# Moving four projections of a two-layer attention kernel from the score loop to the value stage, with narrower bias products and tokens that carry their own ones

## The chip, the cores and the metric

The kernel runs on one core of a Trainium2 chip. The metric is device time in microseconds (us) of one execution, the median of several. The core has a matrix engine (TensorE, "PE" in the profile, with its weight loads listed apart as "PEld"), VectorE ("DVE"), ScalarE ("ACT"), GpSimd ("POOL") and a queue engine that issues transfers ("SP"). TensorE writes its results to PSUM, which is divided into banks of 512 fp32 columns; VectorE and ScalarE read them from there. All data are fp32. A matmul of fp32 shows in the trace as two passes, each with its own weight load.

## The reference, cut to what matters

Sixteen images of 64 x 64 positions and 256 channels go through two layers, each with a residual:

```python
# layer 0: linear attention on the group-normalised input
q, k, v = split(gn(x) @ w_qkv)            # 8 heads of 32
q = softmax(q, over the 32 of a head) * 32**-0.5
k = softmax(k, over all 4096 positions)
context = einsum('bhdn,bhen->bhde', k, v)
x = x + einsum('bhde,bhdn->bhen', context, q) @ w_out

# layer 1: attention in a 7 x 7 window on the group-normalised result
q, k, v = gn(x) @ Wq + bq, gn(x) @ Wk + bk, gn(x) @ Wv + bv
scores = sum over d of q[d] * (unfolded k[d] + emb[d])     # 49 neighbours
x = x + sum over neighbours of softmax(scores) * unfolded v
```

`gn` is a group norm with 32 groups, without scale or shift. `emb` is a position embedding: one half depends on the row offset of the neighbour, the other on its column offset.

## The kernel before, in words

The work of one image comes in three stages. The order of instructions on TensorE, ScalarE, VectorE and SP is the order in which the program writes them (`manual_schedule`, L1170); the instructions of GpSimd are not in that list. A tile framework adds the waits between engines.

**Layer 0** (`layer0`, L576). Sixteen pieces of 256 positions are projected (L592), exponentiated by ScalarE (L596) and summed into a 256 x 257 context per half of the heads (L610). The right side of that product are the *tokens*: the unnormalised input, position by position, with a 257th column of ones, so that the last column of the context is the sum of the keys' exponentials. `load_tokens` (L519) writes the ones with GpSimd (L522) and loads the rest from the array `xt` in HBM (L523); the tokens of an image are loaded in pieces, beside the last attention steps of the image before and during layer 0. Context, value weights and output weights are then multiplied together to one weight per head (L660 to L683); VectorE and ScalarE copy the result from PSUM to `w4` (L707, L708), and the products L733 with these weights give layer 0's output, four heads at a time on four row tiles.

**Values** (L1212 to L1260). The group norm is not applied to the image: its scale is multiplied into the weights (`scale`, L761), and its mean is taken off through the bias. `fold_bias` (L765) computes for each of the five bias columns the product of the scaled weights with the mean (L772) and subtracts it (L774): columns 0 and 1 are the keys', 2 and 3 the queries', 4 belongs to the position products. The position products (L790) are placed by ScalarE, stored to HBM and read back as rings. Then the eight strips of 512 positions get their value products (L854), in the order `KEYED`; VectorE adds the bias (L863), and the result goes to HBM. The loop index over `KEYED` is i = 0 to 7; the bias products of keys and queries stand in i = 2.

The keys and queries of the window attention are made in *jobs*. A key job `("k", hg, s)` makes keys for half `hg` of the heads and strip `s`: 2 matmuls of 512 columns, 4 passes. A query job `("q", hg, t, half)` makes a quarter `t` of the columns, one half of the rows: 6 matmuls of 96 to 256 columns, 12 passes. Both are at L902 (`job_products`, L877). `place_job` (L910) moves a job's bank from PSUM to SBUF with its bias, in one instruction per head (two for strip 0, whose positions lie in two pieces); `evacuate` (L776) does it on ScalarE (L779) or on VectorE (L781). `AHEAD` (L47) names the jobs made among the values, placed by ScalarE; `JOBS` (L48) those made among the attention steps, and `placements` (L82) says, by the remainder of the step number by five, in which step each engine places which heads, ahead of that step's scores (`FIRST`) or behind them (`LAST`).

**Window attention** (`local_attention`, L947). A round k of eight makes one quarter of one half of the heads (`SEQUENCE`); a round has nine chunks in five groups, so 40 steps, with two chunks a step and one in each fifth. Three things run at once, one step apart. In step n, group n gets its scores (L990), and ScalarE exponentiates them (L999 or L1002); the scores of all chunks alternate between two double banks, so a chunk's scores wait for the exponential of the chunk before last. Group n - 1 is multiplied with the values (L1034) into two output banks, `single[0]` and `single[1]`, which are cleared at the start of a round (L1045) and copied by ScalarE at its end (L1133); VectorE then adds the overlap of neighbouring chunks (L1019). Group n - 2 is summed (L1073) into `single[2]`, which VectorE transposes out of the bank (L1079) and inverts (L1081). Jobs use `single[2]` or `single[3]`: a job of step n with n % 5 = 3 stands ahead of the value products and uses `single[3]`; one in `single[2]` stands behind them, and where n % 5 = 0 and there is a job of step n + 1, that one follows it at once in `single[3]`.

So four lists set the order around the change: TensorE's, ScalarE's, VectorE's and SP's. `load_window` (L935) brings the values of a round to SBUF through SP; `load_rings` (L830) the position rings.

Of the kernel before, what the change touches and what calls it, by code (L numbers as in the profile page):

```python
# [19 lines left out]
P = 128  # L20
W = 64
C = 256
HEADS, HD = 8, 32
NS = 8
# [21 lines left out]
SUMS = ((0, 18), (18, 42), (42, 64))  # L46
AHEAD = {3: (("k", 0, 2), ("k", 0, 3)), 4: (("k", 0, 4),), 5: (("q", 0, 1, 0),), 6: (("q", 0, 1, 1),), 7: (("k", 0, 5),)}  # L47
JOBS = {  # L48
    0: ("k", 0, 6),
    1: ("q", 0, 2, 0),  # L50
    2: ("q", 0, 2, 1),
    3: ("k", 0, 7),
    5: ("q", 0, 3, 0),
    6: ("k", 0, 0),
    7: ("q", 0, 3, 1),
    8: ("k", 0, 1),
# [22 lines left out]
FIRST, LAST = 0, 1  # L79


def placements():  # L82

    plan = {}
    for n, job in JOBS.items():
        if job[0] == "k" and job[2] == 0:
            parts = ((0, LAST, 1, (2, 3)), (1, FIRST, 0, (0, 1)))
        elif n == max(JOBS):
            parts = ((0, LAST, 1, (0, 1)), (1, LAST, 1, (2, 3)))
        elif n % 5 == 1:  # L90
            parts = ((0, LAST, 1, (0, 1)), (1, FIRST, 0, (2, 3)))
        elif n % 5 == 3:
            parts = ((1, FIRST, 1, (0, 1)), (2, FIRST, 0, (2, 3)))
        elif n % 5 == 0:
            parts = ((1, FIRST, 1, (0, 1)), (1, FIRST, 0, (2, 3)))
        else:
            parts = ((1, FIRST, 1, (0, 1, 2, 3)),)
        for later, when, engine, heads in parts:
            plan.setdefault((n + later, when), []).append((n, engine, heads))
    return plan  # L100
# [335 lines left out]
def attention_fast(tc, io, ok):  # L436


    nc = tc.nc
    with ExitStack() as ctx:  # L440
# [15 lines left out]
        B = xc.shape[0]  # L456
# [7 lines left out]
        n = Net(tc, cp, io)  # L464
# [54 lines left out]
        def load_tokens(b, q, t0=0, t1=8):  # L519

            t = tokens_of(q)
            nc.gpsimd.memset(t[:, t0:t1, C : C + 1], 1.0)  # L522
            nc.sync.dma_start(t[:, t0:t1, :C], xt[b, q, :, t0:t1])  # L523

# [51 lines left out]
        def layer0(b, x, xn, mean, rstd, ready, midway=None):  # L576
# [128 lines left out]
            w4 = vbuf[0][:, : 8 * C].rearrange("p (h g c) -> p h g c", h=4, g=2)  # L705
            for h in range(2):
                nc.vector.tensor_copy(w4[:, h].rearrange("p g c -> p (g c)"), double[0][:, h])  # L707
            nc.scalar.copy(w4[:, 2:4].rearrange("p h g c -> p h (g c)"), double[1])  # L708
# [56 lines left out]
        def fold_bias(mean, folded, psum):  # L765

            for i, weights in folded:
                for a in range(2 if i == 4 else 1):
                    rows = slice(64 * a, 64 * a + 64) if i == 4 else slice(0, P)
                    for k in range(2):  # L770
                        w = weights[:, k] if i == 4 else weights[:, k, P * (i % 2) : P * (i % 2) + P]
                        nc.tensor.matmul(psum[rows, i : i + 1], w, mean[:, k : k + 1], start=(k == 0), stop=(k == 1))  # L772
            span = slice(folded[0][0], folded[-1][0] + 1)
# [396 lines left out]
        with tc.manual_schedule(engines=ORDERED):  # L1170
# [40 lines left out]
            for b in range(B):  # L1211
# [25 lines left out]
                for i in range(4):  # L1237
                    positional(i, pairs[i])
                spares = iter(single + single[:2])
                for i, s in enumerate(KEYED):  # L1240
# [12 lines left out]
                    if i in (3, 4):  # L1253
                        load_rings(32 * (i - 3), 32 * (i - 2))
                    for job in AHEAD.get(i, ()):
                        bank_of = next(spares)
                        job_products(job, x, bank_of)
                        place_job(job, bank_of, 1)
                    if i == 5:
# [84 lines left out]
def attention_general(tc, io):  # L1344

    nc = tc.nc
    with ExitStack() as ctx:
# [80 lines left out]
        def image(src, tokens, dst):  # L1428
# [35 lines left out]
            for s in range(NS):  # L1464
                xtok = tok.tile([P, 4, C], F32, tag="xtok", name=f"gxtok{s}")
                i = ORDER.index(s)
                nc.sync.dma_start(xtok, tokens[i // 2, :, 4 * (i % 2) : 4 * (i % 2) + 4])
                for hg in range(2):
# [249 lines left out]
```

## Time and profile before

| | us |
|---|---|
| median of 3 runs | 5167.11 (5166.51 to 5168.44) |
| profiled execution | 5175.71 |
| its span, first to last instruction | 5173.9 |

| engine | busy us | share of the span |
|---|---|---|
| PE | 5061.7 | 98% |
| PEld | 3751.8 | 73% |
| DVE | 3013.1 | 58% |
| ACT | 2571.2 | 50% |
| POOL | 1447.9 | 28% |

The granted clock of TensorE was 0.997 over the span. One image takes about 320 us. In one of them the stage from the bias of the position products to the end of the values runs from 1131.3 to 1170.4 us, and the window attention begins at 1170.4. In a timeline a row gives the start, the length of the merged run, engine, line, operation, output and inputs, shape and count; in brackets stands the idle time of that engine before the row and what ended it. Runs of TensorE are pipelined, so a run's length reaches into the next one; its cost is the difference between starts. In a list of waits the numbers are total us, times, and the longest.

### The profile page before, as it was taken

What the parts mean: (1) busy time and instruction counts of PE and PEld (TensorE: products, weight loads), DVE (VectorE), ACT (ScalarE), POOL (GpSimd) and SP (SyncE); (2) the same over time, 40 slices, a digit from 0 to 9 for tenths busy, and PEclk for the clock granted to TensorE, in tenths of its full rate; (3) what the DMA queues carried; (4) which work ended last, traced back from release to release, by engine and by line L of the source; (5) the groups of instructions that cost most, each with busy time, mean ns of one, the idle gap of its engine ahead of it and who ended that gap; (6) DMA issues with size and microseconds to landing.
All of it is one profiled execution on the core that took longest, in us unless ns stands there. A gap on an engine that the chain in (4) does not pass through costs nothing.

```text
span 5173.9 us, 175006 instructions
## 1 busy us (share of the span) xinstructions
PE 5061.7 (98%) x76273; PEld 3751.8 (73%) x76273; DVE 3013.1 (58%) x5754; ACT 2571.2 (50%) x3473; POOL 1447.9 (28%) x2630
## 2 busy tenths in 40 slices
PE   7999999999999999999999999999999999999998
PEld 4776867777677776777767677676776767767676
DVE  5474655646556465564755647556475564755546
ACT  1562735527265372653726537174471744717446
POOL 3041241412414123140331403314042140422404
PEclk9999999999999999999999999999999999999999
DMA  4542525425154351543415434153441534416343
GB/s 132 128 122 52 151 66 123 121 56 150 60 132 117 68 144 50 134 117 76 134 50 137 118 82 133 46 139 111 93 125 44 151 98 103 128 39 150 91 93 90
DMA packets 637705, 537.33 MB, mean 104 GB/s; under 512 B 129585, under 2 KB 570545, under 8 KB 632177
## 3 DMA queue, kind: packets, MB, share of 16 engines
q1 hardware_dynamic: 595712, 515.94, 37.5%
q10 hardware_dynamic: 41216, 10.10, 1.2%
q8 instruction: 602, 9.86, 0.8%
q14 instruction: 175, 1.43, 0.1%
HBM read 367.11 MB, written 158.73 MB: 102 GB/s over the span
## 4 chain that ended last, share of the span: by engine, by line
PE 96%; DVE 2%; issue 1%; POOL 0%; ACT 0%; DMA 0%; SPq 0%; POOLq 0%; ACTq 0%; DVEq 0%
PE ps L902 18%; PE pd L592 17%; PE pd L990 16%; PE ps L1034 9%; PE pd L854 9%; PE ps L610 8%; PE ps L1073 4%; PE ps L733 4%; PE pd L733 4%; PE ps L790 2%; PE ps L1045 1%; PE ps L772 1%; DVE qq L781 0%; PE pd L683 0%; PE pd L1235 0%
## 5 line engine op out<-in xcount | busy, mean ns | idle before, releaser
L779 ACT ACTIVATE qq<-ps,bias 32x512 f32<-32x512 f32 (+2 forms) x928 | 678.8, 737 | 836.9 <-DVE bias L774 649.6
L1019 DVE TENSOR_TENSOR e<-e,e 128x384 f32<-128x384 f32 x1024 | 697.9, 711 | 416.5 <-PE ps L1034 337.3
L592 PE MATMUL pd<-wqkv,img 128*128 128x512 f32 x2048 | 926.9, 595 | 8.3 <-DVE img L363 8.3
L596 ACT ACTIVATE eq<-pd 128x1024 f32<-128x1024 f32 x256 | 262.2, 1024 | 1063.9 <-PE pd L592 1063.9
L990 PE MATMUL pd<-qq,kaug 64*64 64x84 f32 (+5 forms) x24192 | 764.1, 267 | 10.8 <-issue 9.8
L990 PEld LDWEIGHTS pd<-qq,kaug 64*64 64x64 f32 x24192 | 671.4, 133 | 126.6 <-issue 72.4
L505 POOL TENSOR_TENSOR others<-others,turn 128x9 f32<-128x9 f32 (+2 forms) x384 | 86.9, 226 | 2118.6 <-DVE turn L1079 2117.8
L592 PEld LDWEIGHTS pd<-wqkv,img 128*128 128x128 f32 x2048 | 387.4, 190 | 394.2 <-issue 350.1
L599 DVE TENSOR_REDUCE qz<-eq 128x16 f32<-128x512 f32 x256 | 175.6, 686 | 714.0 <-ACT eq L596 709.3
L1002 ACT ACTIVATE e<-pd 128x896 f32<-128x896 f32 (+2 forms) x576 | 467.4, 835 | 234.1 <-PE pd L990 153.7
L779 ACT ACTIVATE kaug<-ps,bias 32x512 f32<-32x512 f32 (+2 forms) x768 | 490.3, 648 | 143.9 <-PE ps L902 80.4
L1034 PE MATMUL ps<-e,vbuf 128*32 128x112 f32 (+1 forms) x18432 | 533.3, 252 | 10.7 <-issue 10.6
L999 ACT ACTIVATE e<-pd 128x896 f32<-128x896 f32 (+2 forms) x576 | 465.4, 834 | 149.3 <-PE pd L990 72.2
L902 PE MATMUL ps<-img,wqn 128*128 128x160 f32 (+2 forms) x3072 | 523.4, 320 | 1.0 <-issue 1.0
L902 PEld LDWEIGHTS ps<-img,wqn 128*128 128x128 f32 x3072 | 470.7, 189 | 73.4 <-issue 15.0
L610 PEld LDWEIGHTS ps<-vbuf,eq 128*128 128x128 f32 x2048 | 385.1, 190 | 155.1 <-issue 100.0
L902 PE MATMUL ps<-img,w 128*128 128x512 f32 x1024 | 496.1, 609 | 1.4
L1108 POOL TENSOR_TENSOR img<-img,r 128x320 f32<-128x320 f32 (+1 forms) x512 | 495.2, 993 | 5.0
L610 PE MATMUL ps<-vbuf,eq 128*128 128x257 f32 x2048 | 489.5, 381 | 4.7 <-ACT eq L596 4.7
L1034 PEld LDWEIGHTS ps<-e,vbuf 128*32 128x32 f32 x18432 | 389.9, 109 | 142.2 <-issue 102.0
L854 PE MATMUL pd<-wvn,img 128*128 128x256 f32 x2048 | 468.2, 382 | 4.0 <-DVE hve L358 4.0
L854 PEld LDWEIGHTS pd<-wvn,img 128*128 128x128 f32 x2048 | 382.9, 190 | 67.8 <-issue 15.3
(146 smaller groups left out, 5672.0 us busy)
## 6 DMA issues: line engine op xcount, KB each, us to landing
vbuf<-vpad SPq DMA_DIRECT2D x1152, 96.0 KB
out<-img SPq DMA_DIRECT2D x256, 256.0 KB
vpad<-v SPq DMA_DIRECT2D x112, 512.0 KB
vbuf<-in_xt SPq DMA_DIRECT2D x158, 256.0 KB
img<-in_xc SPq DMA_DIRECT2D x75, 512.0 KB
img<-in_xc SPq DMA_DIRECT2D x106, 256.0 KB
qq<-pos SPq DMA_DIRECT2D x192, 128.0 KB
vbuf<-in_xt SPq DMA_DIRECT2D x60, 384.0 KB
```

The costliest lines, as they stand in the source:

```text
L592: nc.tensor.matmul(ps[:, t], xn[k][:, n0 : n0 + P], n.wqkv_sb[:, k, : 2 * C], start=(k == 0), stop=(k == 1))
L610: nc.tensor.matmul(pc[hg][:, : C + 1], eq[p][:, t, C + hg * P : C + (hg + 1) * P], tokens_of(p // 4)[:, 2 * (p % 4) + t], start=(p == 0 an ...
L733: nc.tensor.matmul(py[a], w4[rows, h, hg, co * P : (co + 1) * P], qv[rows, 4 * hg + h, 8 * HD * i : 8 * HD * (i + 1)], start=(h == 0 and h ...
L779: nc.scalar.activation(dst, src, AF.Identity, bias=bias)
L854: nc.tensor.matmul(pi[:, t], x[k][:, n0 : n0 + P], wv[:, k], start=(k == 0 and t == 0), stop=(k == 1 and t == 1))
L902: nc.tensor.matmul(dst, (wq if what == "q" else wk)[:, k, hg * P : (hg + 1) * P], part(x[k]), start=(k == 0 and i == 0), stop=(k == 1 and ...
L990: nc.tensor.matmul(to, kaug[pl][rows, u, 8 * c : 8 * c + 8].rearrange("p r w -> p (r w)"), q, start=True, stop=True,)
L999: nc.scalar.activation(e.rearrange("p (a n) -> p a n", a=2), ps[:, :, : 2 * m], AF.Exp)
L1002: nc.scalar.activation(e.rearrange("p (x r) -> p x r", r=hi - lo), src, AF.Exp)
L1019: nc.vector.tensor_tensor(part, part, rows_of(hg, c - 1, before, r0, 8 * c), ALU.add)
L1034: nc.tensor.matmul(dst, stationary, pr, **flags)
L1108: nc.gpsimd.tensor_tensor(yv, xv, by_rows(add[:, :, a - w0 : e - w0], xv), ALU.add)
```

## The change

The tables of jobs change. Four jobs, key strips 6 and 7 and both halves of query quarter 2 of the first half of the heads, are made among the values, each right behind a job that was there already. `AHEAD` now says for each job which engine places it: the first of a step of the loop ScalarE (1), the second VectorE (0). In i = 3, where two jobs stood, the second is now placed by VectorE. The banks are taken in turn: `single` twice and its first two once more. In the attention steps the later jobs move up: query quarter 3 from steps 5 and 7 to 2 and 5, key strip 0 from step 6 to step 3. For a strip 0 in a step with n % 5 = 3 there is a placement rule of its own: VectorE places heads 0 and 1 ahead of the next step's scores, ScalarE heads 2 and 3 behind them.

`fold_bias` writes 32 output rows at a time instead of 128 (or 64 for column 4), the four groups of rows in turn. The ones come with the tokens from HBM, and the GpSimd memset goes. The first of the copies to `w4` is divided between VectorE and ScalarE.

```diff
-AHEAD = {3: (("k", 0, 2), ("k", 0, 3)), 4: (("k", 0, 4),), 5: (("q", 0, 1, 0),), 6: (("q", 0, 1, 1),), 7: (("k", 0, 5),)}
+AHEAD = {
+    3: (("k", 0, 2, 1), ("k", 0, 3, 0)),
+    4: (("k", 0, 4, 1), ("k", 0, 6, 0)),
+    5: (("q", 0, 1, 0, 1), ("q", 0, 2, 0, 0)),
+    6: (("q", 0, 1, 1, 1), ("q", 0, 2, 1, 0)),
+    7: (("k", 0, 5, 1), ("k", 0, 7, 0)),
+}
 JOBS = {
-    0: ("k", 0, 6),
-    1: ("q", 0, 2, 0),
-    2: ("q", 0, 2, 1),
-    3: ("k", 0, 7),
-    5: ("q", 0, 3, 0),
-    6: ("k", 0, 0),
-    7: ("q", 0, 3, 1),
+    2: ("q", 0, 3, 0),
+    3: ("k", 0, 0),
+    5: ("q", 0, 3, 1),
     8: ("k", 0, 1),
...
-        if job[0] == "k" and job[2] == 0:
+        if job[0] == "k" and job[2] == 0 and n % 5 == 3:
+            parts = ((1, FIRST, 0, (0, 1)), (1, LAST, 1, (2, 3)))
+        elif job[0] == "k" and job[2] == 0:
             parts = ((0, LAST, 1, (2, 3)), (1, FIRST, 0, (0, 1)))
...
             t = tokens_of(q)
-            nc.gpsimd.memset(t[:, t0:t1, C : C + 1], 1.0)
-            nc.sync.dma_start(t[:, t0:t1, :C], xt[b, q, :, t0:t1])
+            nc.sync.dma_start(t[:, t0:t1], xt[b, q, :, t0:t1])
...
-            for h in range(2):
-                nc.vector.tensor_copy(w4[:, h].rearrange("p g c -> p (g c)"), double[0][:, h])
+            nc.vector.tensor_copy(w4[:, 0, 0], double[0][:, 0, :C])
+            nc.scalar.copy(w4[:, 0, 1], double[0][:, 0, C:])
+            nc.vector.tensor_copy(w4[:, 1].rearrange("p g c -> p (g c)"), double[0][:, 1])
             nc.scalar.copy(w4[:, 2:4].rearrange("p h g c -> p h (g c)"), double[1])
...
             for i, weights in folded:
-                for a in range(2 if i == 4 else 1):
-                    rows = slice(64 * a, 64 * a + 64) if i == 4 else slice(0, P)
-                    for k in range(2):
-                        w = weights[:, k] if i == 4 else weights[:, k, P * (i % 2) : P * (i % 2) + P]
-                        nc.tensor.matmul(psum[rows, i : i + 1], w, mean[:, k : k + 1], start=(k == 0), stop=(k == 1))
+                first = P * (i % 2) if i < 4 else 0
+                for k in range(2):
+                    for q in range(4):
+                        c0 = first + HD * (q if i < 4 else q % 2)
+                        nc.tensor.matmul(
+                            psum[HD * q : HD * q + HD, i : i + 1],
+                            weights[:, k, c0 : c0 + HD],
+                            mean[:, k : k + 1],
+                            start=(k == 0),
+                            stop=(k == 1),
+                        )
...
-                spares = iter(single + single[:2])
+                spares = iter(single + single + single[:2])
...
-                    for job in AHEAD.get(i, ()):
+                    for *job, engine in AHEAD.get(i, ()):
                         bank_of = next(spares)
                         job_products(job, x, bank_of)
-                        place_job(job, bank_of, 1)
+                        place_job(job, bank_of, engine)
...
-        "xt": np.ascontiguousarray(tiles.transpose(0, 1, 3, 2, 4)),
+        "xt": np.concatenate([tiles.transpose(0, 1, 3, 2, 4), np.ones((B, NS // 2, P, 8, 1), np.float32)], axis=4),
```

More of the change, by code (lines that the diff above doesn't have):

```diff
@@ L1466, in image @@
                 i = ORDER.index(s)
-                nc.sync.dma_start(xtok, tokens[i // 2, :, 4 * (i % 2) : 4 * (i % 2) + 4])
+                nc.sync.dma_start(xtok, tokens[i // 2, :, 4 * (i % 2) : 4 * (i % 2) + 4, :C])
                 for hg in range(2):
```

## The prediction

> **What bounds the kernel now.** I read the page first (busy time, then the chain that ended last), then one image on TensorE's timeline, then the waits, then ScalarE and VectorE around the same instants.
>
> ```profile
> PE 5061.7 (98%) x76273; PEld 3751.8 (73%) x76273; DVE 3013.1 (58%) x5754; ACT 2571.2 (50%) x3473; POOL 1447.9 (28%) x2630
> PE 96%; DVE 2%; issue 1%; POOL 0%; ACT 0%; DMA 0%; SPq 0%; POOLq 0%; ACTq 0%; DVEq 0%
> ```
>
> TensorE is busy 98% and is 96% of the chain. A change can win only by making TensorE's list shorter or removing one of its few pauses, and it loses whatever new pauses it makes. So I price everything in TensorE time, from one image start to the next start (a run's own duration overlaps its successor). One image, TensorE's timeline:
>
> ```profile
> 1140.69 0.95 PE L772 MATMUL ps<-hmean,w 128*128 128x1 f32 x8
> 1141.50 1.03 PE L772 MATMUL ps<-hmean,wqn 128*128 128x1 f32 x8
> 1142.39 3.70 PE L854 MATMUL pd<-wvn,img 128*128 128x256 f32 x16
> ...
> 1152.81 1.88 PE L902 MATMUL ps<-img,w 128*128 128x512 f32 x4
> 1154.53 3.62 PE L854 MATMUL pd<-wvn,img 128*128 128x256 f32 x16
> ...
> 1171.77 1.98 PE L902 MATMUL ps<-img,w 128*128 128x512 f32 x4
> 1173.59 1.99 PE L902 MATMUL ps<-img,wqn 128*128 128x160 f32 x12
> 1175.51 1.57 PE L990 MATMUL pd<-qq,kaug 64*64 64x112 f32 x48
> ...
> 1190.79 0.38 PE L1034 MATMUL ps<-e,vbuf 128*32 128x48 f32 x16
> 1191.10 2.09 PE L902 MATMUL ps<-img,wqn 128*128 128x160 f32 x12
> 1193.02 1.91 PE L902 MATMUL ps<-img,w 128*128 128x512 f32 x4
> 1194.86 1.56 PE L990 MATMUL pd<-qq,kaug 64*64 64x112 f32 x48
> ```
>
> The first two rows are the bias products: 16 passes (each fp32 matmul shows as two) take 1.70 us, 106 ns a pass, for one column each: that is weight loading. The L902 rows are the projections ("jobs"): 1.72 us among the values (1152.81 to 1154.53), 1.82 to 2.02 among the scores, where the array changes its tile shape around them.
>
> ```profile
> DVE kaug L781 <- ACT kaug L779: 137.7, 48, 6.0
> DVE qq L781 <- ACT qq L779: 106.4, 80, 2.1
> PE ps L733 <- DVE vbuf L707: 12.5, 16, 0.8
> ```
>
> When ScalarE and VectorE share the placing of one bank, VectorE waits for ScalarE to end (first two rows): the two halves of a placement run one after the other. The third row is a pause of 0.78 us per image before the output products.
>
> **The change, part by part (per image, 16 images).**
>
> *Bias products.* For keys and queries 8 matmuls become 32, each on a 32-column tile, four tiles in turn: 64 passes for 16. The nearest row with 32-column tiles and few columns is the L1034 row at 1190.79: 16 passes in 0.31 us to the next start, the change of shape at its end included, so at most 19 ns each. Within it four neighbours run at once; 48 columns cost each tile about 42 ns, and one column should cost less. The other side: four 32-column loads take 106/4 = 27 ns if they overlap. So 64 passes are 16 rounds of 27 to 42 ns, 0.43 to 0.67 us; with about 0.2 us for two changes of shape (0.07 to enter, 0.13 to leave, as around L1034) I take 0.75, a gain of 0.95 (0.83 to 1.08). A rule speaks against it: the Trainium skill, "TensorE: Matmul & The Clock Gate", Back-to-back issue gap, gives a floor of about 25 ns to any matmul of 1 to 64 columns. By it 64 x 25 ns + 0.2 = 1.80, a loss of 0.10. The 19 ns row already lies under that floor, so I go by the row and keep the rule as the far end. The position biases (4 matmuls to 8) stay at zero: 8 passes took 0.40 us, 16 half as wide take as much, and VectorE's bias (0.25 us pause before L1235) ends the wait as before.
>
> *First copy of the output weights.* VectorE's first 512 columns (686 ns) become 256 on VectorE (about 0.42, as L1236 at 421 ns) and 256 on ScalarE. TensorE's first products need only VectorE's half: the 0.78 us pause shrinks by 0.27. ScalarE's half, behind VectorE's in the same bank, ends about 0.4 us later, when TensorE has 0.54 us of work on the first half; its next copy (1012 ns) then ends about 0.5 us before it is needed. Gain 0.27; if ScalarE's start slips, 0.
>
> *Tokens.* The ones arrive by DMA, so 14 POOL memsets of 0.1 us per image go; each stood in POOL's queue ahead of the rescaling and waited for window reads. SP issues the same number of loads, 0.4% more bytes in longer runs. TensorE waits for neither; zero. If tokens came late, the context products would wait, but the trace has no such row.
>
> *The jobs.* Before: key strips 6 and 7 and query quarter 2 (two halves) are made in steps 0 to 3; the change makes them among the values and lets the later jobs move up. Steps lose: at step 0, 1.82 + 1.92 and one change of shape (1.36 of scores to L902 at 1171.77, against 1.23 to more scores), 0.15; at step 5, where a query and a key job become one query job, 1.75; at step 7, 2.02. Sum 7.66. The values gain 2 x 1.72 + 2 x 1.83 = 7.09. Gross gain 0.57. VectorE places the four (4 x 0.76 = 3.0 us each) during the next strip's 3.45 us of value products, so values are not held up.
>
> Those jobs also covered other engines. Three waits come due:
>
> ```profile
> 1170.51 2.76 ACT L779 ACTIVATE kaug<-ps,bias 32x512 f32<-32x512 f32 x4 [2.44 <-PE ps L902]
> 1173.30 1.41 ACT L999 ACTIVATE e<-pd 128x512 f32<-128x512 f32 x2
> ```
> ```profile
> 1188.19 0.22 DVE L1081 RECIPROCAL rc<-turn 128x9 f32<-128x9 f32 x1
> 1188.66 1.03 DVE L1019 TENSOR_TENSOR e<-e,e 128x384 f32<-128x384 f32 x2 [0.26 <-PE ps L1034]
> 1189.60 0.58 DVE L1079 STREAM_TRANSPOSE turn<-ps 128x384 f32<-128x384 f32 x1
> ...
> 1194.63 1.52 DVE L781 TENSOR_SCALAR qq<-ps,bias 32x512 f32<-32x512 f32 x2 [2.06 <-ACT qq L779]
> ```
>
> (1) *Steps 0 and 1.* ScalarE places key strip 5 for 2.76 us before the first exponentials. Scores began at 1170.41; the first exponential ends at 1173.30 + 0.60. In the new order 1.72 us of key strip 7 lies in between, so that end is 1.77 us after the scores begin. Scores alone reach the third chunk, which needs that buffer, after 1.23 (0.50 and 0.73 for the two chunks before it, from their starts): wait 0.6, and 0.12 more at the fourth chunk. Queued behind: everything on TensorE. Before, 3.7 us of jobs hid it. **0.73**.
>
> (2) *Step 5.* Key strip 0 moves from step 6 to step 3, and its rule puts VectorE's half first in step 4 (four pieces, 1.71 us where it stands now), ahead of the overlap additions (1188.66) and the transpose that frees the sums bank (to 1190.18). The query job at 1191.10 writes that bank. The transpose ends at 1191.67, the job starts at 1191.73: **0.63**.
>
> (3) *Step 6.* That job's placement (ScalarE 1.37, then VectorE 1.52) must end before the last sums go into the bank. Until now 1.84 us of key job followed; without it TensorE is there 2.45 us after the job's end, and the halves need 3.03. ScalarE also comes late: its half of strip 0 follows VectorE's half (one bank), so exponentials and the two output copies end 0.5 us after the job does. **1.1**.
>
> A second rule weighs here: "PSUM — Partial Sum Buffer", PSUM bank collisions, lets two engines read one bank in different 32-partition quadrants. Under it the halves would overlap and wait 3 would be gone (jobs +0.8 instead of +1.9). The L781 waits say this kernel serialises by bank; I go by them. That ScalarE also waits for VectorE, in that order, no row shows.
>
> Jobs: 7.09 - 7.66 + 0.73 + 0.63 + 1.1 = +1.89. Instruction supply: TensorE has rare pauses marked "issue" on the scores (some 20 us in the run); denser steps and 112 more instructions, 0 to 0.3, I take 0.1.
>
> **Sum:** 1.89 - 0.95 - 0.27 + 0.10 = +0.77 us per image, x16 = +12.3. The profiled execution took 5175.7 (span 5173.9) and would take 5188; the same added to the runs' median, 5167.1, is **5179.5**.
>
> **The rivals.**
> - *The step 4 to 6 waits halve* because ScalarE need not wait for VectorE or the halves overlap: 0.5 to 1.1 less, +0.3 to -0.3; middle about 5168. For it: quadrants differ. Against: 128 waits of VectorE on ScalarE.
> - *Faster.* The sums bank is never waited for in steps 5 and 6: 1.73 less, -0.96 x 16 = -15, 5152. It decides at two points: VectorE's half of strip 0 would have to take under 1.1 us, or stand behind the transpose, and the query's halves under 2.4 us together. Against: 1.71, and 2.9.
> - *Bias products gain nothing* (the 25 ns rule, or fetching instructions for 64 short passes): +1.05 x 16 = 17 more, 5196.
> - *Nothing moves*: the jobs' gross gain is only 0.57 and TensorE's list is otherwise equal; this is the first rival's number.
>
> **How the numbers follow.** A difference under 0.2% (10 us) is what a measurement here can hardly tell from none. Main case 0.55 (5171 to 5188; above 5177.4 in three of four), halved waits 0.22 (mostly within 0.2%), faster 0.10, no bias gain 0.13. Slower 0.41 + 0.02 + 0.13 = 0.56; faster 0.09; same 0.35. The range 5158 to 5197 leaves out the faster rival and the far end of the dearest, about 0.15 to 0.2; the likeliest case's own range is 5171 to 5188.
>
> **What would show it.** In the changed profile: L772 for keys and queries as 64 passes in 0.6 to 0.9 us; TensorE's pause at L733 down from 0.78 to about 0.5; new rows of TensorE waiting for ScalarE's exponentials (L999) of about 0.7 us at step 1, for VectorE's transpose (L1079) of 0.6 at a query job in step 5, and for VectorE's placement (L781) of 1.1 at the sums (L1073) in step 6, each 16 times. The prediction is wrong if those rows are missing, if L772 stays near 1.7 us, or if the value products wait for VectorE's placements.

## The result, and the profile after

The changed kernel takes 5190.32 us (median of 4 runs, 5187.94 to 5196.36); the kernel before took 5167.77 us beside it. The ratio is 1.0040, with a 95% interval of 1.0028 to 1.0053: slower by 22.5 us (14 to 27 by the interval), where the prediction had 12.3. The profiled execution took 5196.4 us (span 5194.5), 20.7 us more than the profiled one of before; both lie above the medians of their kernels, by 6 and 8 us.

The busy times of the changed kernel:

```profile
PE 5050.5 (97%) x77169; PEld 3721.2 (72%) x77169; DVE 3181.5 (61%) x5978; ACT 2422.6 (47%) x3265; POOL 1453.5 (28%) x2410
```

TensorE works 11 us less than before (5050.5 against 5061.7) and the kernel still ends 21 us later. So the loss lies in TensorE's pauses. VectorE has 168 us more to do and ScalarE 149 us less: part of the placing went from one to the other.

The chain that ended last can't be followed in the changed kernel's profile: it breaks off at GpSimd's last instructions.

TensorE's timeline in the same image as the one shown of before (start, duration, engine, line, operation; in brackets the idle time ahead and what ended it):

```profile
1140.77 0.43 PE L776 MATMUL ps<-hmean,w 128*32 128x1 f32 x32
1141.04 0.44 PE L776 MATMUL ps<-hmean,wqn 128*32 128x1 f32 x32
1141.41 3.72 PE L864 MATMUL pd<-wvn,img 128*128 128x256 f32 x16
...
1158.74 3.84 PE L912 MATMUL ps<-img,wqn 128*128 128x160 f32 x24
1162.42 3.65 PE L864 MATMUL pd<-wvn,img 128*128 128x256 f32 x16
...
1178.41 1.86 PE L1000 MATMUL pd<-qq,kaug 64*64 64x112 f32 x48 [0.39 <-ACT e L1009]
...
1193.93 0.52 PE L1044 MATMUL ps<-e,vbuf 128*32 128x48 f32 x16
1194.94 2.09 PE L912 MATMUL ps<-img,wqn 128*128 128x160 f32 x12 [0.49 <-DVE turn L1089]
...
1198.78 0.81 PE L1044 MATMUL ps<-e,vbuf 128*32 128x64 f32 x32
1200.47 0.81 PE L1083 MATMUL ps<-e,ones 128*32 128x128 f32 x24 [0.88 <-DVE qq L791]
...
1209.01 0.97 PE L1044 MATMUL ps<-e,vbuf 128*32 128x112 f32 x32
1210.14 0.86 PE L1083 MATMUL ps<-e,ones 128*32 128x128 f32 x24 [0.16 <-DVE turn L1089]
```

The bias products now go from 1140.77 to 1141.41, 0.64 us for 64 passes where 16 took 1.70. Then come the three waits that the prediction named: at the scores of step 1, at the query job of step 5, at the sums of step 6. The last two rows are a fourth that it did not name: the sums of step 9 start 1.13 us after the products ahead of them. The kernel before needs 0.79 there:

```profile
1207.85 0.97 PE L1034 MATMUL ps<-e,vbuf 128*32 128x112 f32 x32
1208.64 0.84 PE L1073 MATMUL ps<-e,ones 128*32 128x128 f32 x24
```

TensorE's waits, summed over the run (total us, times, longest):

```profile
PE ps L1083 <- DVE qq L791: 14.2, 16, 0.9
PE ps L912 <- DVE turn L1089: 9.8, 16, 0.6
PE ps L737 <- DVE vbuf L709: 8.3, 16, 0.6
PE ps L1083 <- DVE turn L1089: 6.8, 23, 0.9
PE pd L1000 <- ACT e L1009: 6.2, 16, 0.4
```

Four of the rows come sixteen times, once per image. The fourth row mixes the wait of step 9 with others of the same kind (the kernel before has 4.9 us there, 14 times). The third row is the pause at the output weights; the kernel before had it at 12.5. In these rows a wait counts only while the array is idle, so each time lost is a little more than its row. The table below takes it from the distance between the starts of TensorE's runs instead, as a mean over 15 images. Each row is the difference of the changed kernel from the kernel before at that place, counted from the start of the image (the position biases' bias products):

```
place in an image                                   difference, us   the prediction's steps up to there
start of step 0's scores                              +6.13            +7.09 - 0.95 = +6.14
start of step 1's products (wait 1)                   +2.98            +3.0
start of step 6's products (wait 2)                   +1.89            +1.9
start of step 11's products (wait 3, then step 9)     +1.31            +0.9
start of the output products (first copy)             +0.91            +0.8
next image                                            +1.28            +0.77
```

Until step 6 the forecast holds to 0.1 us. It falls short by 0.4 us between steps 6 and 11 and by 0.3 to 0.4 us from the output products to the next image; between these two places about 0.25 us came back, which the experiment on the tokens bears on. Of the 0.37 us behind the output products' start, 0.27 is the first copy (see its experiment); the other 0.10 stands ahead of the position biases, whose products begin 0.10 us later behind the position products when they write 32 rows at a time, in the changed kernel and with the bias products alone. They end 0.06 us sooner, so this place costs 0.04 where the prediction had zero.

VectorE's and ScalarE's waits for each other at the placements:

```profile
DVE qq L791 <- ACT qq L789: 111.9, 64, 3.3
DVE kaug L791 <- ACT kaug L789: 42.7, 32, 2.7
```
```profile
ACT kaug L789 <- DVE kaug L791: 24.8, 16, 1.6
```

The last row is new: ScalarE waits 1.55 us per image for VectorE's half of key strip 0, which now stands first.

### The profile page after: what moved, and what is told of

Read it like the earlier page. It is cut to its first block, busy times and chain, and to the rows that moved or that the text cites. A ratio compares the mean times of both kernels' runs of the same rounds, so it can differ in the third digit from the quotient of the medians.

```text
span 5194.5 us, 176637 instructions
## 1 busy us (share of the span) xinstructions
PE 5050.5 (97%) x77169; PEld 3721.2 (72%) x77169; DVE 3181.5 (61%) x5978; ACT 2422.6 (47%) x3265; POOL 1453.5 (28%) x2410
## 5 line engine op out<-in xcount | busy, mean ns | idle before, releaser
L789 ACT ACTIVATE qq<-ps,bias 32x512 f32<-32x512 f32 (+1 forms) x832 | 613.7, 744 | 888.3 <-DVE bias L784 639.2
L789 ACT ACTIVATE kaug<-ps,bias 32x512 f32<-32x512 f32 (+2 forms) x640 | 403.4, 642 | 196.3 <-PE ps L912 110.9
L791 DVE TENSOR_SCALAR kaug<-ps,bias 32x512 f32<-32x512 f32 (+2 forms) x512 | 341.7, 677 | 152.6 <-PE ps L912 69.8
```

The costliest lines, as they stand in the source:

```text
L789: nc.scalar.activation(dst, src, AF.Identity, bias=bias)
L791: nc.vector.tensor_scalar(dst, src, bias, None, ALU.add)
```

## The experiments

Each kernel is timed against the kernel before on the same chip; a number of us over or under the kernel before is the difference of the two medians. Where two kernels' intervals overlap, as those of the changed kernel and of most of its variants do, the trace decides and not the time.

**One part alone.** Four kernels, each the kernel before with one part of the change.

First the bias products:

```diff
+                first = P * (i % 2) if i < 4 else 0
+                for k in range(2):
+                    for q in range(4):
+                        c0 = first + HD * (q if i < 4 else q % 2)
...
```

> The kernel before with the new bias products alone. Theory (the traces of before and after): the 64 short passes take 0.64 us where 16 took 1.70, the neighbouring runs lose 0.11, so 0.95 us per image less, and up to 0.06 at the position biases: 15 to 16 us under the kernel before. Rival (what is saved there is given back at the next wait, or the 25 ns floor of the rule holds once the cover of the jobs is gone): within 3 us of the kernel before.

Measured: 5161.52 us, 8.9 under the kernel before; ratio 0.9982 (0.9973 to 0.9990). Its TensorE timeline around the products, in the same image:

```profile
1131.52 0.43 PE L772 MATMUL ps<-hmean,w 128*32 128x1 f32 x32
1131.79 0.44 PE L772 MATMUL ps<-hmean,wqn 128*32 128x1 f32 x32
1132.16 3.72 PE L860 MATMUL pd<-wvn,img 128*128 128x256 f32 x16
```

0.64 us again. TensorE is 1.0 us ahead of the kernel before at the start of the first step, and still 0.9 to 1.1 ahead at steps 6 and 11 and at the next image; its profiled execution is 14.9 us shorter than that of before. The timed gain is smaller than 15, with an interval of 5 to 14 us. So the expected time was missed by a little, while every place in the trace has about the full microsecond. The 14.9 of the two profiled executions can't settle it, since the one of before was itself 5.3 us slower than the median it is compared with. Where the remainder goes is not shown; pauses that differ from run to run (see the tokens) may be part of it. The rival, no gain, is out.

Then the jobs, with their banks and placements:

```diff
-    0: ("k", 0, 6),
-    1: ("q", 0, 2, 0),
-    2: ("q", 0, 2, 1),
-    3: ("k", 0, 7),
-    5: ("q", 0, 3, 0),
-    6: ("k", 0, 0),
-    7: ("q", 0, 3, 1),
+    2: ("q", 0, 3, 0),
+    3: ("k", 0, 0),
+    5: ("q", 0, 3, 1),
...
```

> The kernel before with the moved projections and their placements alone. Theory: gross gain 0.57 per image, three waits of 0.70, 0.70 and 1.07, and the wait of the sums in step 9 for VectorE's transpose, 0.39, together +2.3 per image: 36 us over the kernel before (30 to 40), with all four waits at their sizes of the changed kernel. Rival A (the step 9 wait does not come from the jobs): +1.9, 30 us, and no wait at step 9. Rival B (one of the waits comes from the shorter bias products, which bring the whole stage forward): under 25 us.

Measured: 5209.18 us, 38.8 over the kernel before; ratio 1.0073 (1.0059 to 1.0086). All four waits are there. At the start of step 11's products it is 2.24 us per image behind the kernel before, times 16 is 36 us. (Its profiled execution was its fastest, 5200.0 us, and at the next image only 1.49 behind; the difference arises in the later steps.) Rival A would be 0.39 per image less, and rival B falls because the waits have the same size without the shorter bias products. The jobs cost more than the whole change does; the other parts win some of it back.

The first copy of the output weights:

```diff
-            for h in range(2):
-                nc.vector.tensor_copy(w4[:, h].rearrange("p g c -> p (g c)"), double[0][:, h])
+            nc.vector.tensor_copy(w4[:, 0, 0], double[0][:, 0, :C])
+            nc.scalar.copy(w4[:, 0, 1], double[0][:, 0, C:])
+            nc.vector.tensor_copy(w4[:, 1].rearrange("p g c -> p (g c)"), double[0][:, 1])
```

> The kernel before with the split first copy of the output weights alone. Theory: the pause ahead of the output products shrinks from 0.78 to 0.52 us, but VectorE's next copy waits for ScalarE's half and TensorE for that copy, so the stage as a whole gains nothing: within 2 us of the kernel before, with the wait of TensorE for the second copy 16 times at 0.4 us. Rival (the prediction's own step): 0.27 per image less, 4.3 us.

Measured: 5170.22 us, 0.2 under the kernel before; ratio 0.9998 (0.9990 to 1.0006). The stage begins 0.26 us earlier and is 0.27 us longer. In the kernel before VectorE makes its two copies without a wait between them:

```profile
1408.62 1.29 DVE L707 COPY vbuf<-pd 128x512 f32<-128x512 f32 x2 [0.67 <-PE pd L683]
```

The copies and the weight load behind them, in the changed kernel:

```profile
1412.03 0.43 DVE L709 COPY vbuf<-pd 128x256 f32<-128x256 f32 x1 [0.67 <-PE pd L686]
1412.49 0.37 ACT L710 COPY vbuf<-pd 128x256 f32<-128x256 f32 x1 [6.90 <-DVE vbuf L709]
...
1412.90 0.69 DVE L711 COPY vbuf<-pd 128x512 f32<-128x512 f32 x1 [0.44 <-ACT vbuf L710]
...
1413.64 2.47 PEld L737 LDWEIGHTS ps<-qq,vbuf 32*128 32x128 f32 x48 [0.39 <-DVE vbuf L711]
```

The three copies run in a chain: VectorE, ScalarE, VectorE. VectorE is idle for 0.44 us until ScalarE's half is done, although its second copy reads other columns of that pair of banks, and TensorE's next weight load waits 0.39 us for that copy. What was won ahead of the first product was lost about a microsecond later. The rows show that the copies were kept in this order; whether the program's framework or the hardware asked for it, they don't show.

The tokens with their ones:

```diff
-            nc.gpsimd.memset(t[:, t0:t1, C : C + 1], 1.0)
-            nc.sync.dma_start(t[:, t0:t1, :C], xt[b, q, :, t0:t1])
+            nc.sync.dma_start(t[:, t0:t1], xt[b, q, :, t0:t1])
...
```

> The kernel before with the tokens' ones brought by the transfer instead of GpSimd's memset, alone. Theory (the prediction's step): no change, within 2 us; TensorE never waits for tokens. Rival (the transfers of the tokens, now with longer rows, land later or disturb the instruction fetches): up to 5 us slower, with more idle time of TensorE marked as issue.

Measured: 5164.88 us, 5.5 under the kernel before; ratio 0.9990 (0.9983 to 0.9996). Neither theory had a gain. In the trace it lies in the last steps of an image, up to step 39, which is where the next image's tokens are loaded: from the clearing of the output banks in step 36 to the next image's first projection TensorE takes 9.72 us on average, against 10.47 before, and the longest of 15 images takes 10.5 against 13.4.

**Which half of the tokens' edit?** The new transfer has fewer and longer packets; the memset is gone from GpSimd's queue. This kernel keeps the memset ahead of the new transfer (shown against the kernel with the tokens alone):

```diff
+            nc.gpsimd.memset(t[:, t0:t1, C : C + 1], 1.0)
             nc.sync.dma_start(t[:, t0:t1], xt[b, q, :, t0:t1])
...
```

> The kernel before with the tokens and their ones in one long row per transfer, and GpSimd's memsets kept ahead of them. It tells apart what made the tokens' part alone faster. Theory (fewer and longer packets, 600 thousand in place of 638 thousand, leave TensorE's instruction fetches less delayed while the tokens load, in the last steps): the gain stays, 4 to 7 us under the kernel before, the last stretch of steps (35 to 39) at 9.7 us a mean image in place of 10.2 to 10.7. Rival (the memsets in GpSimd's queue cost the time): no gain, within 2 us of the kernel before.

Measured: 5173.62 us, 4.8 over the kernel before; ratio 1.0012 (1.0003 to 1.0021). With the memset back there is no gain, so the packets alone don't bring it. Neither theory had it slower than before. Its load writes over the memset's column and so has to come after it, but that is no difference from the kernel before, where SP holds the loads back for the memsets too, as often and about as long. SP's waits in the kernel before, then with the memset kept:

```profile
SPq L523 <- POOL vbuf L522: 669.3, 123, 12.4
```
```profile
SPq L523 <- POOL vbuf L522: 650.2, 123, 12.4
```

With the tokens alone these waits are gone, and the loads wait for the readers of their buffer directly. Why the time is 4.8 us over the kernel before stays open; the profiled execution, 5165.8 us, was one of its fastest and doesn't show it. In that execution the last steps take 10.17 us, with the other kernels that have memsets (10.21 to 10.74). TensorE's idle time there for which the profile names no engine ("issue"), summed over 15 images:

```
with the memsets:     before 12.3, bias alone 15.4, copy alone 14.0, jobs alone 9.5, memset kept 10.5 us
without the memsets:  tokens alone 5.7, changed kernel 6.9, the seven other kernels built on either 2.7 to 5.9 us
```

The two groups don't overlap. Of the memsets the profile of before shows, in its view of that tile (idle time of GpSimd ahead of them, until what):

```profile
L522 POOL MEMSET vbuf<- x220: 92/102/123, 2.4 to 4884.5; 128x2 f32 x79, 128x3 f32 x30, 128x8 f32 x1
...
  PE ps L1034: 29.3, 15
```

GpSimd stood still ahead of a memset for about 2 us per image, waiting for TensorE to finish with a window. What TensorE waits for in the pauses can be read from the transfers in the trace, which the views above don't join to them. The page of the kernel before lists among its transfers (packets, MB, share of the 16 engines):

```profile
q8 instruction: 602, 9.86, 0.8%
```

Over the whole run this kernel has 29 such pauses, and every one ends 1.2 to 1.7 us after one of these 16 KB packets of instructions has landed; in the changed kernel it is 33 of 34. Of TensorE's matmuls at large (every 97th) only 7 to 8% start at that distance. This points to waits for instructions as what the pauses are. How the memsets make them longer was not found: the instruction transfers in the last steps take as long with the memsets (1.03 us on average before) as without (1.07 for the tokens alone).

**Step 5 and step 6.** In the changed kernel, key strip 0 is placed by VectorE first, then ScalarE, in step 4. Here ScalarE comes first, and VectorE's half only at step 7:

```diff
-            parts = ((1, FIRST, 0, (0, 1)), (1, LAST, 1, (2, 3)))
+            parts = ((1, LAST, 1, (2, 3)), (4, FIRST, 0, (0, 1)))
```

> The changed kernel, with key strip 0 (made in step 3) placed by ScalarE behind the scores of step 4 and by VectorE only at step 7, in place of VectorE first in step 4. Theory: the wait of the step 5 query job for VectorE's transpose (0.70 per image) goes, since VectorE's 1.7 us no longer stand ahead of the transpose; the wait of the sums in step 6 falls from 1.07 to about 0.5, because ScalarE is no longer late but the two halves of the query's placement still run one after the other; the step 9 wait stays. About 1.2 per image, 19 us under the changed kernel, some 3 us over the kernel before (-2 to +8). Rival (the step 6 wait is due to the two halves alone): 0.70 per image, 11 us under the changed kernel, 11 over the kernel before.

Measured: 5176.86 us, 3.9 over the kernel before (the changed kernel: 22.5); ratio 1.0011 (1.0004 to 1.0019). In the trace, the wait of step 5 is gone (0.68 per image), and the sums of step 6 wait 0.34 less, at this row:

```profile
1191.57 0.81 PE L1083 MATMUL ps<-e,ones 128*32 128x128 f32 x24 [0.55 <-DVE qq L791]
```

So of the wait of 1.07 in step 6 about a third was ScalarE being late and the rest is the two halves one after the other. When and in which order the two halves of one small placement are made is worth 16 us by the trace and about 19 by the times, of the change's 22.5.

Next, the query job in the other single bank, so that it need not share the bank of the sums:

```diff
-    5: ("q", 0, 3, 1),
+    6: ("q", 0, 3, 1),
...
-            parts = ((1, FIRST, 0, (0, 1)), (1, LAST, 1, (2, 3)))
+            parts = ((1, LAST, 1, (2, 3)), (2, FIRST, 0, (0, 1)))
...
-                    if step % 5 == 0 and step + 1 in JOBS:
-                        job_products(JOBS[step + 1], x, single[3])
+                if step % 5 == 0 and step + 1 in JOBS:
+                    job_products(JOBS[step + 1], x, single[3])
```

> The changed kernel, with the query job of step 5 made in the other single bank (not the one of the sums) and placed from step 6 on; key strip 0 placed by ScalarE behind the scores of step 4 and by VectorE at the start of step 5. Theory: both waits on the sums bank go (0.70 and 1.07 per image), the step 0 and 1 wait (0.7) and the step 9 wait (0.4) stay: 28 us under the changed kernel, about 6 us under the kernel before (0 to -12). Rival (what is removed comes back one step later, at the transposes or the sums): no more than 15 us under the changed kernel, 7 or more over the kernel before.

Measured: 5186.81 us, 13.9 over the kernel before; ratio 1.0034 (1.0021 to 1.0047). The theory fell and its rival holds: the wait came back at the same job. VectorE and TensorE at that place:

```profile
1190.88 0.58 DVE L1089 STREAM_TRANSPOSE turn<-ps 128x384 f32<-128x384 f32 x1
...
1191.64 1.69 DVE L791 TENSOR_SCALAR kaug<-ps,bias 32x320 f32<-32x320 f32 x4
```
```profile
1192.02 0.46 PE L1044 MATMUL ps<-e,vbuf 128*32 128x48 f32 x16
1193.48 2.06 PE L912 MATMUL ps<-img,wqn 128*128 128x160 f32 x12 [1.00 <-DVE kaug L791]
```

The other bank holds key strip 0, and VectorE empties it only behind its transposes, up to 1193.33. The query job could have started at 1192.48. Whichever bank it takes, it waits for a placement: with its 1.7 us ahead of the transposes VectorE holds up the one bank, and behind them the other.

Last, the query job left in step 7, where the kernel before has it, with no job in step 5:

```diff
-    5: ("q", 0, 3, 1),
+    7: ("q", 0, 3, 1),
```

> The changed kernel with the query job of step 5 left in step 7, where the kernel before has it, placed by ScalarE alone in step 8. Theory: the wait for the transpose in step 5 and that for the placement in step 6 go (0.70 and 1.07 per image), and since a job stands in step 7 again GpSimd's work on the first round is over before the additions of step 8, so the step 9 wait goes too (0.39): 2.16 per image, 35 us under the changed kernel, about 12 under the kernel before (-5 to -18). Rival (the job in step 7 meets the sums bank of its own, or the placement in step 8 holds up the exponentials): no more than 20 us under the changed kernel.

Measured: 5183.47 us, 14.7 over the kernel before; ratio 1.0032 (1.0020 to 1.0044). The expectation fell: the waits of steps 5, 6 and 9 are all gone, but a new one of 1.35 us stands ahead of the scores of step 6, for the exponentials. ScalarE and TensorE there:

```profile
1187.76 1.74 ACT L789 ACTIVATE kaug<-ps,bias 32x320 f32<-32x320 f32 x4 [1.55 <-DVE kaug L791]
1189.52 1.41 ACT L1009 ACTIVATE e<-pd 128x512 f32<-128x512 f32 x2
```
```profile
1188.44 0.38 PE L1044 MATMUL ps<-e,vbuf 128*32 128x48 f32 x16
1190.17 1.70 PE L1000 MATMUL pd<-qq,kaug 64*64 64x112 f32 x48 [1.35 <-ACT e L1009]
```

ScalarE waits 1.55 us for VectorE's half of key strip 0, then places its own for 1.74, and only then makes the exponentials that TensorE's scores need. In the changed kernel the query job of step 5 had stood in front of that. The rival's number held, at another place than the one it named. The kernel that has both edits, this one and ScalarE's half first, was not tried.

**Steps 0 and 1.** Here VectorE places both of the last two key strips among the values, in the two single banks that step 1 leaves free, and ScalarE is idle when the scores begin:

```diff
-    7: (("k", 0, 5, 1), ("k", 0, 7, 0)),
+    7: (("k", 0, 5, 0), ("k", 0, 7, 0)),
...
-                spares = iter(single + single + single[:2])
+                spares = iter(single[2:] + single + single)
```

> The changed kernel, with key strips 5 and 7 (the last two jobs among the values) both placed by VectorE, in the two single banks that are not needed in step 1. Theory: ScalarE is free for the first exponentials, so the wait of steps 0 and 1 goes (0.73 per image): 12 us under the changed kernel, about 11 over the kernel before, and no row of TensorE waiting for the exponentials. Rival (VectorE's 6 us of placing hold up its overlap additions, which the sums need in step 3): the wait only moves to VectorE's additions, within 4 us of the changed kernel.

Measured: 5203.36 us, 30.4 over the kernel before; ratio 1.0064 (1.0047 to 1.0080). Two things happened. The new rotation of banks gave the first jobs a bank that ScalarE was still emptying of the position products: 0.88 us per image, a cost of the experiment's own. And the wait of steps 0 and 1 stayed, all but 0.12 us: from the first scores to the clearing of the output banks TensorE takes 3.34 us in place of 3.46. ScalarE and TensorE's weight loads there:

```profile
1176.19 3.60 ACT L1009 ACTIVATE e<-pd 128x512 f32<-128x512 f32 x4 [6.71 <-PE pd L1000]
```
```profile
1176.84 0.72 PEld L1000 LDWEIGHTS pd<-qq,kaug 64*64 64x64 f32 x24 [0.18 <-ACT e L1009]
1177.90 0.72 PEld L1000 LDWEIGHTS pd<-qq,kaug 64*64 64x64 f32 x24 [0.34 <-ACT e L1009]
```

ScalarE has stood idle for 6.71 us and starts as soon as the first scores are there; its exponentials then follow each other with a gap of 0.15 us behind the first and none after, 0.60 us for the first and 0.92 for each after it, and TensorE, with two buffers for scores, waits for them. Neither theory had this. The wait is the exponentials' own time; the placement ahead of them only shifted it. The jobs that the kernel before has between these scores are what hid it.

**Step 9.** The changed kernel's VectorE and GpSimd around the fourth wait:

```profile
1207.74 1.95 DVE L1029 TENSOR_TENSOR e<-e,e 128x384 f32<-128x384 f32 x2 [2.20 <-PE ps L1044]
1209.61 0.47 DVE L1089 STREAM_TRANSPOSE turn<-ps 128x288 f32<-128x288 f32 x1
```
```profile
1203.64 3.03 POOL L1104 TENSOR_TENSOR r<-r,r 128x512 f32<-128x512 f32 x2 [1.09 <-DVE r L1096]
1206.63 3.59 POOL L1118 TENSOR_TENSOR img<-img,r 128x320 f32<-128x320 f32 x4
```

In the kernel before GpSimd was done with the first round when VectorE came to these additions:

```profile
1206.58 1.03 DVE L1019 TENSOR_TENSOR e<-e,e 128x384 f32<-128x384 f32 x2 [2.04 <-PE ps L1034]
```
```profile
1202.93 3.58 POOL L1108 TENSOR_TENSOR img<-img,r 128x320 f32<-128x320 f32 x4
```

In the changed kernel two overlap additions take 1.95 us while GpSimd works on the first round. One experiment leaves GpSimd's work on that round out:

```diff
-                for j in range(2):
+                for j in range(2 if k else 0):
                     if hg == 0:
...
```

> The changed kernel without GpSimd's rescaling and adding for the first of the eight attention rounds (that part of the attention is left out of the output). Theory (the step 9 wait comes from VectorE's overlap additions of step 8, slowed to twice their time by GpSimd's work on the same round): the sums of step 9 no longer wait for the transpose, 0.39 per image, 6 us under the changed kernel, about 16 over the kernel before, and the two overlap additions of step 8 take 1.0 us again in place of 1.95. Rival (VectorE is late in step 8 because its whole list comes later): the wait stays, within 2 us of the changed kernel.

Measured: 5181.34 us, 12.6 over the kernel before and so 9.9 under the changed kernel; ratio 1.0029 (1.0017 to 1.0042). VectorE at the same place:

```profile
1204.76 1.03 DVE L1029 TENSOR_TENSOR e<-e,e 128x384 f32<-128x384 f32 x2 [3.72 <-PE ps L1044]
1205.70 0.47 DVE L1089 STREAM_TRANSPOSE turn<-ps 128x288 f32<-128x288 f32 x1
```

The additions are back at 1.03 us and the sums of step 9 start 0.79 us after the products, in every image, as in the kernel before. The theory holds. (The sums account for about 6 of the 9.9 us; the rest is not attributed.) The trace of the changed kernel also shows how the slowing works. An addition of this shape during which GpSimd does nothing takes 0.54 to 0.56 us, in 526 cases. Of the 325 that start while GpSimd is rescaling or adding, with more than 0.15 us still to go, 323 end 0.41 or 0.42 us after that GpSimd instruction has ended: the addition stands still until the instruction that was there first is over. That the kernel with the query job in step 7 also has 0.79 fits: its last job of that group gives GpSimd time to end before step 8.

**What is left when the jobs stay.** The kernel before with the new bias products and tokens, and the first copies of the output weights split but all on VectorE:

```diff
-            for h in range(2):
-                nc.vector.tensor_copy(w4[:, h].rearrange("p g c -> p (g c)"), double[0][:, h])
+            for g in range(2):
+                nc.vector.tensor_copy(w4[:, 0, g], double[0][:, 0, g * C : (g + 1) * C])
+            nc.vector.tensor_copy(w4[:, 1].rearrange("p g c -> p (g c)"), double[0][:, 1])
```

> The changed kernel with the jobs left where the kernel before has them, and the split copy of the output weights all on VectorE: bias products, tokens and copy alone. Theory: the three parts that gain add up, 9 to 15 for the bias products, 4 to 6 for the tokens, 3 for the copy: 16 to 24 us under the kernel before, about 5150, and under every other kernel of this study. Rival (the gains are taken back by the pauses of the instruction supply, which are random in size): no more than 10 us under the kernel before.

Measured: 5153.32 us, 15.5 under the kernel before; ratio 0.9970 (0.9958 to 0.9982). It is the fastest of all, just short of the 16 to 24 that were expected (9 to 22 by the interval). TensorE's first output product comes as early as with the change's own split, and the stage behind it is 0.07 us longer than with the bias products alone, where the change's own split makes it 0.27: the split pays 0.2 us per image once no copy waits for another engine.

One kernel joins this copy to the other bank and to VectorE's key strips in the changed kernel:

> The changed kernel with all of these together: query job of step 5 in the other bank, key strips 5 and 7 placed by VectorE, and the first copies of the output weights split but all on VectorE. Theory: 1.77 and 0.73 per image of waits go, and 0.22 at the output weights is won since no copy waits for the other engine: 43 us under the changed kernel, about 21 under the kernel before (5149; -14 to -27), with the step 9 wait the only new one left. Rival (waits only move): not under the kernel before.

Measured: 5192.97 us, 20.1 over the kernel before; ratio 1.0046 (1.0029 to 1.0063). Waits only moved: it has the 1.0 us wait for key strip 0, the bank that ScalarE still held, and the exponentials of step 1. Its VectorE at the output weights shows the copies in one piece:

```profile
1414.45 0.76 DVE L710 COPY vbuf<-pd 128x256 f32<-128x256 f32 x2 [0.67 <-PE pd L686]
...
1415.12 0.68 DVE L711 COPY vbuf<-pd 128x512 f32<-128x512 f32 x1
```

The stage of the output products is 0.20 us shorter there than in the changed kernel.

## Why the prediction was right, and where it was short

The direction and the likeliest case's mechanism were right; the sum was 0.51 us per image (8 us) short of the profiled difference of 1.28, and 10 us short of the timed one. The measured 5190.3 lies inside the stated range and just above the likeliest case's own, 5171 to 5188. (5167.1 and 12.3 make 5179.4, not 5179.5; the other sums come out to 0.01.)

- *Bias products, 0.95.* Right in the trace: 0.64 us for the run, 0.11 lost at its neighbours, 0.95 won. (By the times alone 8.9 us, 0.56 per image. The position biases, held at zero, cost 0.04.) 64 passes in 0.64 us are 10 ns each. Trainium skill, "TensorE: Matmul & The Clock Gate", Back-to-back issue gap, with 25 ns per pass would have made 1.6 us of it; on four 32-column tiles in turn this trace disagrees, and the 19 ns row was the right guide.
- *Jobs: 7.09 gained by the values, 7.66 lost by the steps.* Right: the scores begin 6.13 us later, 6.14 forecast with the bias products.
- *The three waits, 0.73, 0.63 and 1.1.* Right in place and size: 0.73, 0.70 and 1.07. For the first, the reason given was half wrong. "ScalarE places key strip 5 for 2.76 us before the first exponentials" accounts for 0.12 us; the rest is the exponentials' own pace, which shows up as soon as nothing stands between the scores. For the second the reason held: without VectorE's half in front, the wait went. For the third, the step had 0.6 for the two halves and 0.5 for ScalarE's lateness; the runs show 0.73 and 0.34.
- *What the prediction could not show:* "That ScalarE also waits for VectorE, in that order, no row shows." It does, by 1.55 us in each image at key strip 0, and all three waits came at full size. So the rival "the waits halve" is out. These rows show the order of this kernel's waits; they don't show whether the hardware could have served both engines at once.
- *Where a stall goes: "the change makes them among the values and lets the later jobs move up".* This step stopped at step 6. With the query job gone from step 7, GpSimd's work on the first round falls on VectorE's additions of step 8, and the sums of step 9 pay 0.34 us in most images, 0.39 on average, 6 us in all. The prediction followed TensorE, VectorE and ScalarE past the moved jobs, not GpSimd.
- *First copy of the output weights, 0.27, "its next copy then ends about 0.5 us before it is needed".* Wrong: 0. That next copy was VectorE's second too, and it waited for ScalarE's half. The price of the slip was in the step as its other end, "if ScalarE's start slips, 0", but the copy that slipped was VectorE's.
- *Tokens, zero.* Wrong: alone they gain 5.5 us (2 to 9). It goes with the memsets; no row has TensorE waiting for tokens or memsets, as the step said, but it left out the pauses of the last steps. How the two are tied is open.
- *Instruction supply, 0.1.* It can't be told from zero: idle time marked "issue" on TensorE differs between 16 and 27 us from profile to profile.

Put together with the measured parts alone: +38.8 for the jobs, -8.9, -0.2 and -5.5 for the others, is +24.2, beside 22.5 measured for all. Three terms of the forecast's sum were wrong, and with opposite signs: step 9 and the copy add 0.66 us per image, the tokens take 0.34 off. That is 0.32 of the 0.51; the second wait and the position biases add 0.1, and the rest is not attributed. So the total came out nearer than its terms, and that was luck.

## What to carry to other kernels

A job that is moved out of a dense stage takes its time off that stage's list, and it uncovers every other engine's work that ran beneath it: write down, for each engine, what it does during the job, GpSimd's long work too, and whose turn comes next. Here a gross gain of 9 us uncovered four waits of 46 us together. Splitting a copy between two engines gained nothing here, because a later copy was queued on the same buffer; splitting it on one engine kept 0.2 us of the gain per image.

## What the runs showed of the hardware that was not expected

- Two elementwise additions of VectorE (128x384) took 1.95 to 2.11 us beside GpSimd's tensor work and 1.03 without it; each that met a GpSimd instruction ended 0.41 or 0.42 us after it, in 323 of 325 cases.
- TensorE's pauses that no engine ends follow a transfer of instructions at 1.2 to 1.7 us, in 29 of 29 cases before and 33 of 34 after.
- 64 one-column fp32 passes on 32-column tiles took 0.64 us, with 128-row weights for each: less than half of the 1.70 us for 16 passes with 128-column weights.
- GpSimd memsets of 0.1 us that wait in its queue for TensorE go with more of these pauses: 9.5 to 15.4 us in the last steps of 15 images with them, 2.7 to 6.9 without. Why is open.
